# Layer 1's aggregation by pairs of panels: seven block products, weights behind each panel, clamp and residual on ScalarE

## The chip, the cores and the metric

The kernel runs on one NeuronCore of a Trainium2 chip. The metric is device time in microseconds (us) of one execution. The engines are named as the profile names them: PE (TensorE, matmul), DVE (VectorE), ACT (ScalarE), POOL (GpSimd) and SP (SyncE). ACT, POOL and SP also issue DMA transfers, each from a queue of its own that works in order.

## The reference

Two layers, each a graph aggregation followed by a mixture of experts with two of eight experts per node. There are 3327 nodes of 256 features in float32, and `adj` is 3327 x 3327 with about 0.24% of its entries nonzero, plus the diagonal.

```python
def _L1_gnn_ref(h, adj, simlar, W_proj, b_proj, W_gcn, b_gcn):   # simlar is adj
    sim = jnp.tanh(adj * simlar)
    filt = sim * (adj > 0).astype(sim.dtype)
    ...                                  # keep the 700 largest of a row
    h2 = jnp.tanh(h @ W_proj + b_proj)
    return jax.nn.relu(new_adj @ (h2 @ W_gcn) + b_gcn)
...
x = x + _L0_gnn_ref(_layernorm(x), adj, ...)     # relu(adj @ (x @ W) + b)
x = x + _L0_ffn_ref(_layernorm(x), ...)          # 8 experts, top 2, relu
x = x + _L1_gnn_ref(_layernorm(x), adj, adj, ...)
x = x + _L1_ffn_ref(_layernorm(x), ...)          # tokens + 8 experts, top 2, gelu
```

The last line adds its input twice: the experts of layer 1 return the normalized tokens plus the experts' sum, and x is added to that. So layer 1's x becomes x + xn before the outputs of the experts are added; this is called the residual below.

## The kernel before, in words

The nodes are padded to 3328: 26 tiles of 128, or 13 panels of 256. The transposed adjacency lies in memory as 13 panels of 256 columns, each panel in two pieces of 128 x 3328 (13 blocks of 128 rows each). Six places in SBUF, `ring`, hold pieces while they are used; `load_pieces` issues their loads on SP's queue in the order of `LOADS`, and the experts later use the same places for blocks of tokens and weights.

**Layer 0** (`aggregate_first`) aggregates the normalized features themselves and applies the weights afterwards: for every finished panel `weigh` (L506) does two matmuls a tile, then `add_relu` (L403, L404) adds bias and x on DVE. Panels 0 and 1 run together, panel 12 alone, and the ten between run as five pairs in `pair` (L571). Two panels, two halves of the nodes and two halves of the features make a 2 x 2 block product; `pair` does it with seven products of 13 matmuls each (L470) instead of eight, with sums of the features (`sum_features`, four DVE operations, once) and sums of pieces (`add_pieces`, L480, sixteen DVE operations a pair). While a pair runs, the panels of the pair before are weighed among the first product's matmuls, normalized, routed (`route`: DVE scores, L662) and listed (`listed`: tokens scattered to the experts' lists by POOL, small PE products L770 and L771). The normalized tiles come from ACT (L360).

**Between the layers** (`between`, L1635) each group of two tiles has the outputs of layer 0's experts added and is normalized on DVE (L1419, L337 to L371), transposed on PE (L387), copied by ACT, projected on PE (L1623) with tanh on ACT (L1630), and multiplied by the second weight in `node_features` (L395); ACT copies the result into `s` (L398). Behind the last normalized tiles the first pieces of layer 1 are filtered: DVE clamps a piece at zero (L1668), ACT squares it and takes tanh in quarters (L1672, L1673).

**Layer 1** (`aggregate`, L430) takes the 13 panels one at a time: 52 matmuls against `s` (L440), `add_relu`, then `after1`: list the panel before, normalize (DVE), scores (DVE; by PE for the last panel), and x + xn on POOL (L1690). `filter_chunk` filters each later piece when it is loaded: clamp on DVE (L1659), Square and Tanh on ACT (L1660, L1661). The exponential of the routing weights is ACT's too (L729).

**Experts of layer 1** run in steps: transposes (L1172), hidden layer (L1226), activation (ACT, L1234), output product (L1323), scaling on DVE (L1330, L1331), scatter to `ys` by POOL (L793). `first_blocks` starts with lists that `plan_early` closed after panel `EARLY_PANS[1]` (9 before). Once the outputs of the first experts are all written, an inner loop (L1762) loads them back while later steps run: `load_outputs` (L1405) on SP's queue, behind the loads of the next step's tokens and weights (L1136, L1143), then `add_loaded` on DVE (L1419) and the store of finished tiles on ACT's queue (L1769). The last tiles are stored at L1803.

Within an engine, instructions run in the order in which the program's scheduler left them; `behind(...)` and `tc.issue_after(...)` place an instruction later in that order.

Of the kernel before, what the change touches and what calls it, by code (L numbers as in the profile page):

```python
# [57 lines left out]
EARLY_PANS = 8, 9  # L58
# [9 lines left out]
def late_order(fixed, spread):  # L68
# [19 lines left out]
SIDE = 2  # L88
UNITS = (
    [(pan,) for pan in range(SIDE)] + [(pan, pan + 1) for pan in range(SIDE, NPAN - 1, 2)] + [(NPAN - 1,)],  # L90
    [(pan,) for pan in range(NPAN)],
# [36 lines left out]
def gnn_moe_two_layers(  # L128
# [262 lines left out]
    def node_features(i, lhsT, w_sb):  # L391

        ps = psy.tile([P, D], F32, name="ps_s", tag="py")
        for c in range(DC):
            nc.tensor.matmul(  # L395
                ps, lhsT=lhsT[:, c, :], rhs=w_sb[:, c, :], start=(c == 0), stop=(c == DC - 1)
            )
        nc.scalar.copy(s[:, i, :], ps)  # L398

# [29 lines left out]

    def aggregate(b_sb, prepare, after):  # L430

        load_pieces(RING - 2 * NCHUNK, prepare)
        for pan in range(NPAN):
            chunks = [piece(pan, k) for k in range(NCHUNK)]
            ps = [psy.tile([P, D], F32, name="ps_g", tag="py") for _ in range(PW // P)]
            for k in range(NCHUNK):
                for it in range(PW // P):
                    for c in range(CJ):
                        j = k * CJ + c
                        nc.tensor.matmul(  # L440
                            ps[it],
                            lhsT=chunks[k][:, c, ts(it, P)],
                            rhs=s[:, j, :],
                            start=(j == 0),
                            stop=(j == NT - 1),
                        )
            for it in range(PW // P):
                add_relu(x[:, pan * (PW // P) + it, :], ps[it], b_sb)
            after(pan)
            load_pieces(NCHUNK, prepare)  # L450
# [31 lines left out]
    def aggregate_first(b_sb, w, w_sb, begin, count, route, listed, freed):  # L482

        sums, waiting, copied, counts = {}, [], [], []
        units = UNITS[0]
# [22 lines left out]

        def finish():
            if not waiting:
                return
            todo = list(waiting)
            waiting.clear()
            if todo[0][0] < NPAN - 1:
                listed()
            for pan, g in todo:
                for it in range(PW // P):  # L520
                    weigh(pan, g, it)
            if todo[0][0] == NPAN - 1:
                listed()
            for _ in route([pan for pan, _ in todo]):
                pass
# [17 lines left out]
        def count_next():  # L543
            if counts:
                count(*counts.pop(0), copied)
# [11 lines left out]

        def rest(pan, first, hooks=(), behind_=BEHIND):
            hooks = dict(hooks)
            for j in range(first, NT):  # L560
                add(pan, j)
                if j == first + behind_:
                    finish()
                if j in hooks:
                    hooks[j]()
            g = sums_of()
            for c in range(DC):
                copy(g[:, c, :], sums[pan][c])
            waiting.append((pan, g))

        def pair(p1, p2, ps_x, ps_q, ps_b, ps_z):  # L571
            a11, a12, a21, a22 = (piece(pan, k) for pan in (p1, p2) for k in range(NCHUNK))
            b11, b21, b22 = half(0, 0), half(1, 0), half(1, 1)
            t3, t2, t4, t1 = half_sums
            hooks, pans = finishing()
            product(ps_x, b11, a11, hooks=hooks)
            g1, g2 = sums_of(), sums_of()
            copy(g1[:, 0, :], ps_x)
            add_pieces(a11, a21)
            add_pieces(a21, a22)  # L580
            count_next()
            listed()
            product(ps_q, t4, a22)
            copy(g2[:, 0, :], ps_q)
            routing = route(pans)
            next(routing)
            add_pieces(a22, a11)
            count_next()
            product(ps_b, b21, a12)
            nc.vector.tensor_tensor(g1[:, 0, :], g1[:, 0, :], ps_b, ALU.add)  # L590
            add_pieces(a12, a22)
            next(routing)
# [9 lines left out]
            count_next()  # L602
# [9 lines left out]

        expect(LOADS[0][SIDE:])
        counts.extend(LOADS[0][:SIDE])
        loads(2)
# [3 lines left out]
        loads(2)  # L619
        with tc.issue_after(last_piece[0].ins):  # L620
            turn_gate(f1_rT)
        for pan in range(SIDE):
            start(pan)
        for j in range(0, CJ, 2):
            for pan in range(SIDE):
                for i in range(j, min(j + 2, CJ)):
                    add(pan, i)
        for _ in range(SIDE):
            count_next()
        for pan in range(SIDE):  # L630
            free(pan, 0)
        for pan in range(SIDE):
            if pan == 1:
                begin(pan)
                sum_features()
            count_next()
            rest(pan, CJ)
            free(pan, 1)
        for _ in range(NCHUNK * SIDE):
            count_next()  # L640
        banks = [psy.tile([P, PW], F32, name="ps_g", tag="py") for _ in range(4)]
        for u in units[SIDE:-1]:
            begin(u[0])
            pair(*u, *banks)
            banks.append(banks.pop(0))
        sums[NPAN - 1] = banks[0:2]
        for _ in range(NCHUNK):
            count_next()
        rest(NPAN - 1, 0, {CJ: layer0.turn_first}, LAST_BEHIND)
        return finish  # L650

# [68 lines left out]
    def weights(sc, n, bias=None, now=False):  # L720


        if bias is not None:
            nc.vector.tensor_tensor(sc, sc, bias.unsqueeze(1).to_broadcast([P, n, E]), ALU.add)
        sel, top, both = top_two(sc, n)
        d = work.tile([P, n], F32, name="rt_d", bufs=2)
        nc.vector.tensor_tensor(d, top[:, :, 1], top[:, :, 0], ALU.subtract)
        if now:
            nc.scalar.activation(d, d, AF.Exp)  # L729
            return sel, both, shares(d, n)  # L730
        return sel, both, d
# [9 lines left out]
    def normalized(t, n, on_scalar=False):  # L741

        stats = statistics(t, n)
        if not on_scalar:
            return [layernorm(t + at, 2, stats, at) for at in range(0, n, 2)]
        shift = shifted(*stats, n)
        xns = [work.tile([P, 2, K, RW], F32, name="xn") for _ in range(0, n, 2)]
        for g in range(n):
            scaled(xns[g // 2][:, g % 2, 0, 0:D], t + g, g, stats[1], shift)
        return xns  # L750
# [4 lines left out]
    def list_waiting():  # L755
        while routed:
            list_tokens(*routed.pop(0))

    def list_tokens(xns, sel, both, w, t0, n, xlist, group):

        if group == "0":
            nc.scalar.activation(w, w, AF.Exp)
# [10 lines left out]
        if group == "0":  # L773
            w = shares(w, n)
# [629 lines left out]
    def load_outputs(yt, ys, t0, n, written, group=None):  # L1404
        d = nc.sync.dma_start(  # L1405
# [102 lines left out]
    def route0(pans):  # L1508
# [7 lines left out]
        routed.append((xns, *weights(sc, n, f0_bg_sb), t, n, xlist0, "0"))  # L1516

    def listed0():
        if not routed or len(routed) == 1 and routed[0][4] == 0:
            return  # L1520
        last = routed[-1][4] + routed[-1][5]
# [17 lines left out]
    layer0.step(None, between=finish_last)  # L1539
    layer0.step(None)  # L1540
# [76 lines left out]
    def second_features(t, xnT):  # L1617
# [13 lines left out]
        second.append(h2)  # L1631
        for g in range(n):
            node_features(t + g, h2T[:, :, ts(g, P)], g1_wg_sb)
# [22 lines left out]
    def filter_chunk(pan, k, a):  # L1656

        with behind(normal if pan == ahead else ()):
            nc.vector.tensor_scalar(a, a, 0.0, None, ALU.max)  # L1659
        nc.scalar.activation(a, a, AF.Square)  # L1660
        nc.scalar.activation(a, a, AF.Tanh)  # L1661
# [21 lines left out]
    def after1(layer1, pan):  # L1683
# [4 lines left out]
        routed.append((xns, *weights(sc, n, now=True), t, n, xlist1, "1"))  # L1688
# [8 lines left out]
    def panels1(layer1, turn=False):  # L1697


        def after(pan):  # L1700
            if pan < NPAN - 1:
                after1(layer1, pan)
                if turn and pan == NPAN - 2:
                    layer1.turn_first()
            else:
                list_waiting()

        return after

    def first_blocks(layer1):  # L1710
# [6 lines left out]
        layer1.step(None)  # L1717
        layer1.step(None)
        with tc.issue_after(last_product[0].ins):
            after1(layer1, NPAN - 1)  # L1720
        layer1.step(None)
# [10 lines left out]
    with tc.If(first_usual > 0) as arms:  # L1732
# [14 lines left out]
        aggregate(gnn_b_sb, filter_chunk, panels1(layer1, True))  # L1747
        late1 = first_blocks(layer1)
# [13 lines left out]
        with tc.If(second_usual > 0) as inner:  # L1762
# [8 lines left out]
            while len(layer1.started) < layer1.always:  # L1771
# [11 lines left out]
                if waiting and at > waiting[0][1] + (1 if k < FIRST_TILES // 2 else 2):  # L1783
                    tiles, _, written = waiting.pop(0)
                    yt = ring[k % RING][:, PIECE - 2 * K * D :].rearrange("p (n d) -> p n d", n=2)
                    load_outputs(yt, ys1, *tiles, written, "read1")
# [21 lines left out]
    with arms.Else():  # L1808
# [11 lines left out]
        with tc.If(most_reg > TOPK) as many:  # L1820
            with tc.tile_pool(name="topk", bufs=1) as tk:
                topk_rows(tc, tk, ring, psy, pst, adj, s, x, gnn_b_sb, ident, filtered, add_relu)
            for pan in range(NPAN):
                panels1(layer1)(pan)
        with many.Else():
# [4 lines left out]
            aggregate(gnn_b_sb, filter_chunk, panels1(layer1))  # L1830
        rows_written.extend(first_arm)
        early_rows.extend(first_arm)
        layer1.rest(first_blocks(layer1))
# [3 lines left out]
def topk_rows(tc, pool, places, psy, pst, adj, s, x, b_sb, ident, filtered, add_relu):  # L1837
# [8 lines left out]
    with tc.For_i(0, NT, 1) as i:  # L1846
# [49 lines left out]
        ps = psy.tile([P, D], F32, name="ps_k", tag="py")  # L1896
        for j in range(NT):
            nc.tensor.matmul(
                ps, lhsT=fT[:, j, :], rhs=s[:, j, :], start=(j == 0), stop=(j == NT - 1)
            )  # L1900
# [75 lines left out]
```

## Time and profile before

| | |
|---|---|
| device time, median of 3 runs | 1191.62 us (1187.46 to 1192.87) |
| profiled execution | 1192.74 us; span 1191.0 us, mean granted PE clock 0.989 |
| aggregation of layer 0, one pair | 43.02 us |
| first product of layer 1's aggregation | 748.68 us |
| one panel of layer 1 | 22.65 us |
| last product of layer 1's aggregation ends | 1043.8 us |
| last product of the experts ends | 1171.8 us |

Times inside an execution count from the start of its span. A row of a timeline gives start, duration, engine, line, operation, output and inputs, how many instructions were merged, and in brackets how long the engine had been idle before it and what ended that. A row of the windows gives, for a stretch of time, the busy time of each engine with the number of its instructions, then the clock granted to PE (1.00 is full), the busy share of the DMA engines and their GB/s. A row of the groups by form gives a line's instructions of one shape, their number, busy time, the mean of one in ns, and the idle time before them.

### The profile page before, as it was taken

How to read it: one execution, taken by the hardware profiler on the slowest of the kernel's cores; microseconds unless marked ns; L12 is line 12 of the kernel's file. 1: busy time of each engine (PE TensorE's matmuls, PEld its weight loads, DVE VectorE, ACT ScalarE, POOL GpSimd, SP SyncE). 2: the span in 40 equal slices, each digit the busy share in tenths (PEclk: the TensorE clock that was granted, in tenths of full speed). 3: DMA queues.
4: the chain of work that ended last, by engine and by line, in shares of the span. 5: the costliest groups of instructions: out<-in, count | busy, mean ns of one | idle time of the engine just before them, and what ended most of it. 6: DMA issues, size and time to landing. Idle time of an engine off the chain costs nothing. (4 is left out here: it accounts for less than half of the span.)

```text
span 1191.0 us, 19704 instructions
## 1 busy us (share of the span) xinstructions
PE 1152.0 (97%) x6217; PEld 1005.4 (84%) x6217; DVE 867.1 (73%) x3001; ACT 557.0 (47%) x1051; POOL 290.5 (24%) x367
## 2 busy tenths in 40 slices
PE   8999999999899999999999999999999999999973
PEld 7888888888788888888888888888888888888852
DVE  6698999988885555454545669289999998785454
ACT  5599647540233333434333346985455562043321
POOL 2111332242331112111111010022232232265531
PEclk9999999999999999999999999999999999999996
DMA  9896738724376555757565955145354451479696
GB/s 349 180 265 260 241 127 239 257 88 152 125 260 224 195 186 187 270 182 258 199 219 168 386 208 201 65 183 180 144 204 166 161 200 55 134 229 273 202 288 207
DMA packets 123185, 241.68 MB, mean 203 GB/s; under 512 B 24480, under 2 KB 93120, under 8 KB 116160
## 3 DMA queue, kind: packets, MB, share of 16 engines
q1 hardware_dynamic: 108656, 205.59, 52.7%
q0 software_dynamic: 11136, 31.60, 7.2%
q10 hardware_dynamic: 3280, 3.15, 0.8%
q8 instruction: 51, 0.84, 0.3%
q14 instruction: 62, 0.51, 0.1%
HBM read 203.98 MB, written 36.33 MB: 202 GB/s over the span
## 5 line engine op out<-in xcount | busy, mean ns | idle before, releaser
L440 PE MATMUL ps_g<-s,ring 128*128 128x256 f32 x1352 | 294.2, 380 | 0.0
L440 PEld LDWEIGHTS ps_g<-s,ring 128*128 128x128 f32 x1352 | 256.0, 190 | 34.4
L1234 ACT ACTIVATE pad<-ps_h,ring 128x256 f32<-128x256 f32 (+1 forms) x282 | 128.9, 458 | 287.2 <-PE ps_h L1226 156.1
L1226 PE MATMUL ps_h<-pad,ring 128*128 128x256 f32 (+1 forms) x1184 | 254.4, 367 | 4.4 <-ACT pad L1176 4.1
L1226 PEld LDWEIGHTS ps_h<-pad,ring 128*128 128x128 f32 x1184 | 200.9, 190 | 46.7 <-ACT pad L1234 11.1
L662 DVE SCALAR_TENSOR_TENSOR rt_product<-xn,gate 128x256 f32<-128x256 f32 x400 | 194.9, 487 | 16.1 <-ACT xn L360 2.8
L793 POOL DMA_INDIRECT ys<-pad,index x114 | 115.7, 1015 | 363.8 <-DVE pad L1281 236.1
L793 POOL DMA_INDIRECT xlist<-xn,rt_idx x104 | 115.0, 1106 | 156.9 <-DVE ln_nw L347 60.9
L1495 ACT ACTIVATE sign<-ring,below 128x416 bf16<-128x416 f32 x208 | 133.4, 641 | 13.8 <-DMA ring<-in_adjT 7.8
L470 PE MATMUL ps_g<-ring,pad 128*128 128x256 f32 x520 | 115.1, 380 | 0.8 <-DMA ring<-in_adjT 0.8
L470 PEld LDWEIGHTS ps_g<-ring,pad 128*128 128x128 f32 x520 | 98.4, 190 | 14.4 <-DMA ring<-in_adjT 1.2
L1660 ACT ACTIVATE ring<-ring 128x3328 f32<-128x3328 f32 x22 | 65.4, 2979 | 87.3 <-DVE ring L1659 56.2
L1281 DVE SCALAR_TENSOR_TENSOR pad<-ps_y,ring,pad 128x128 f32<-128x128 f32 x176 | 59.3, 348 | 47.5 <-PE ps_y L1274 47.3
L470 PE MATMUL ps_g<-ring,s 128*128 128x256 f32 x390 | 89.6, 379 | 0.0
L470 PEld LDWEIGHTS ps_g<-ring,s 128*128 128x128 f32 x390 | 74.1, 190 | 10.1
L480 DVE TENSOR_TENSOR ring<-ring,ring 128x768 f32<-128x768 f32 (+1 forms) x80 | 79.7, 1014 | 0.0
L495 PE MATMUL ps_g<-ring,s 128*128 128x256 f32 x312 | 70.2, 386 | 4.4 <-ACT s L360 4.4
L495 PEld LDWEIGHTS ps_g<-ring,s 128*128 128x128 f32 x312 | 60.1, 194 | 13.5 <-ACT s L360 5.2
L1661 ACT ACTIVATE ring<-ring 128x3328 f32<-128x3328 f32 x22 | 65.4, 2979 | 0.6
L1265 DVE TENSOR_TENSOR xnT<-pad 128x512 f32<-128x512 f32 x22 | 15.2, 692 | 59.2 <-ACT pad L1234 59.2
L1323 PE MATMUL ps_y<-ring,pad 128*128 128x256 f32 x224 | 53.8, 386 | 0.0
L776 POOL COPY xn<-rt_w 128x4 f32<-128x4 f32 x26 | 4.8, 198 | 197.8 <-DVE rt_w L738 197.8
(240 smaller groups left out, 1584.3 us busy)
## 6 DMA issues: line engine op xcount, KB each, us to landing
ring<-in_adjT SPq DMA_DIRECT2D x50, 1664.0 KB, 8.2
ring<-in_f_w1T SPq DMA_DIRECT2D x30, 1024.0 KB, 5.7
ring<-in_f_w2T SPq DMA_DIRECT2D x30, 1024.0 KB, 8.0
ring<-xlist SPq DMA_DIRECT2D x52, 258.0 KB, 3.5
ring<-in_f_w SPq DMA_DIRECT2D x36, 256.0 KB, 3.8
ring<-ys SPq DMA_DIRECT2D x12, 512.0 KB, 4.2
ring<-in_f_b SPq DMA_DIRECT2D x34, 128.0 KB, 7.6
xlist<-h2T SPq DMA_DIRECT2D x16, 257.0 KB, 7.8
```

What stands on the lines that cost most here:

```text
L440: nc.tensor.matmul(ps[it], lhsT=chunks[k][:, c, ts(it, P)], rhs=s[:, j, :], start=(j == 0), stop=(j == NT - 1),)
L470: nc.tensor.matmul(ps, lhsT=b[:, c, :], rhs=a[:, c, :], start=(first and c == 0), stop=(c == CJ - 1), skip_group_check=not first,)
L480: nc.vector.tensor_tensor(out[:, part, :], out[:, part, :], other[:, part, :], ALU.add)
L495: nc.tensor.matmul(sums[pan][c], lhsT=s[:, j, ts(c, P)], rhs=piece(pan, j // CJ)[:, j % CJ, :], start=(j == 0), stop=(j == NT - 1),)
L662: nc.vector.scalar_tensor_tensor(product, xn, 1.0, gate[:, e, :], ALU.mult, ALU.mult, accum_out=sc[:, g, e : e + 1],)
L793: d = nc.gpsimd.indirect_dma_start(out=a[:, :], out_offset=bass.IndirectOffsetOnAxis(ap=index, axis=0), in_=rows_, in_offset=None,)
L1226: last_product[:] = [nc.tensor.matmul(ps, lhsT=w1[:, c, ts(hc, P)], rhs=xT[:, c, :], start=(c == 0), stop=(c == DC - 1),)]
L1234: nc.scalar.activation(hT[:, hc, :], ps, func, bias=bb1[:, hc : hc + 1])
L1281: last_y[:] = [nc.vector.scalar_tensor_tensor(part, ps, xb[:, g, WT : WT + 1], part, ALU.mult, ALU.add)]
L1495: nc.scalar.activation(sign, piece(pan, k)[:, :, ts(i, GROUP)], AF.Sign, bias=below, accum_out=positive[:, pan, i, k : k + 1],)
L1660: nc.scalar.activation(a, a, AF.Square)
L1661: nc.scalar.activation(a, a, AF.Tanh)
```

## The change

It has seven parts.

1. `aggregation` is cut out of `aggregate_first`, and `aggregate_second` uses it for layer 1: panels 0 to 9 as five pairs, panels 10, 11 and 12 alone. The aggregated thing is h2 itself; `weigh` multiplies by the weight behind each panel, so `second_features` transposes h2 back by tiles (four transposes and one copy for two tiles) where `node_features` multiplied. `sum_features` runs for layer 1 too.
2. In the first pair (`begun`) the product of b21 and a12 comes second and the one of t4 and a22 third; the other pairs keep layer 0's order.
3. `filter_piece` clamps on ACT (Relu), then Square and Tanh; of one piece in each pair DVE clamps half.
4. In pairs ACT writes the normalized tiles and also x + xn (`twice`: x scaled by the inverse deviation plus one); panels alone keep DVE and POOL.
5. Routing is spread: `route1` is a generator, the exponential moves to `shares_begun`, lists are done one at a time (`list_next`) at set places (`LIST_AT`, `FURTHER_AT`); the last panel is weighed and routed inside the first three expert steps. `EARLY_PANS` is 8, 8. Panels 11 and 12 take their scores from PE. At the end of layer 0's aggregation the second-last list moves behind the first expert step.
6. The inner loop's `load_outputs` goes to ACT's queue.
7. `topk_rows`, an arm that these inputs don't take, is fitted to the new order of products.

```diff
-EARLY_PANS = 8, 9
+EARLY_PANS = 8, 8
...
-SIDE = 2
+SIDE, ALONE = 2, 3
+LIST_AT, FURTHER_AT = (6, 22, 14), (12, 12, 18)
 UNITS = (
...
-    [(pan,) for pan in range(NPAN)],
+    [(pan, pan + 1) for pan in range(0, NPAN - ALONE, 2)] + [(pan,) for pan in range(NPAN - ALONE, NPAN)],
 )
...
+        def pair(p1, p2, ps_x, ps_q, ps_b, ps_z, filtering=False, begun=False):
...
+            def second_sum():
+                product(ps_q, t4, a22)
+                copy(g2[:, 0, :], ps_q)
+
+            def first_output():
+                product(ps_b, b21, a12)
+                nc.vector.tensor_tensor(g1[:, 0, :], g1[:, 0, :], ps_b, ALU.add)
+
...
+            if begun:
+                first_output()
+            else:
+                second_sum()
             routing = route(pans)
-            next(routing)
+            next(routing, None)
+            if begun:
+                second_sum()
             add_pieces(a22, a11)
             count_next()
-            product(ps_b, b21, a12)
-            nc.vector.tensor_tensor(g1[:, 0, :], g1[:, 0, :], ps_b, ALU.add)
+            if not begun:
+                first_output()
...
+    def aggregate_second(b_sb, w_sb, count, route, listed, freed, turn_first=None):
+
+        a = aggregation(UNITS[1], b_sb, w_sb, count, route, listed, freed)
+        a.loads(RING - 2 * NCHUNK)
+        sum_features()
+        banks = banks_of_pairs()
+        pairs = [u for u in UNITS[1] if len(u) == 2]
+        for u in pairs:
+            a.pair(*u, *banks, filtering=True, begun=u is pairs[0])
+            banks.append(banks.pop(0))
+        for i, pan in enumerate(range(NPAN - ALONE, NPAN)):
...
+            hooks[BEHIND] = weighed
+            hooks[LIST_AT[i]] = listed
+            hooks[FURTHER_AT[i]] = further
+            hooks[NT - 3] = ended
...
+        if twice:
+            more = work.tile([P, n], F32, name="ln_more", bufs=2)
+            nc.vector.tensor_scalar(more, stats[1], 1.0, None, ALU.add)
+            for g in range(n):
+                scaled(x[:, t + g, :], t + g, g, more, shift)
...
+        pt = psy.tile([P, n, D], F32, name="ps_s", tag="py")
         for g in range(n):
-            node_features(t + g, h2T[:, :, ts(g, P)], g1_wg_sb)
+            for c in range(DC):
+                nc.tensor.transpose(pt[:, g, ts(c, P)], h2T[:, c, ts(g, P)], ident)
+        nc.scalar.copy(s[:, t : t + n, :], pt)
...
-    def filter_chunk(pan, k, a):
-
-        with behind(normal if pan == ahead else ()):
-            nc.vector.tensor_scalar(a, a, 0.0, None, ALU.max)
-        nc.scalar.activation(a, a, AF.Square)
-        nc.scalar.activation(a, a, AF.Tanh)
+    def filter_piece(pan, k, copied):
+
+        a = piece(pan, k).rearrange("p c w -> p (c w)")
+        shared = pan < NPAN - ALONE and pan % 2 == 0 and k == 1
+        parts = [a[:, 0 : PIECE // 2], a[:, PIECE // 2 :]] if shared else [a]
+        if shared:
+            nc.vector.tensor_scalar(parts[1], parts[1], 0.0, None, ALU.max)
+        with behind(copied):
+            nc.scalar.activation(parts[0], parts[0], AF.Relu)
+            nc.scalar.activation(a, a, AF.Square)
+            nc.scalar.activation(a, a, AF.Tanh)
...
-                    load_outputs(yt, ys1, *tiles, written, "read1")
+                    load_outputs(yt, ys1, *tiles, written, "read1", nc.scalar)
```

## The prediction

> **What bounds the kernel now.** I read the page's busy times first, then the busy time by stage, then the seams in the timelines.
>
> The page, busy time of each engine:
>
> ```profile
> PE 1152.0 (97%) x6217; PEld 1005.4 (84%) x6217; DVE 867.1 (73%) x3001; ACT 557.0 (47%) x1051; POOL 290.5 (24%) x367
> ```
>
> TensorE (PE) sets the time nearly everywhere. The windows show where another engine is close behind (a layer-0 pair; the end of the stage between the layers; two stretches of layer 1's aggregation; the last expert steps):
>
> ```profile
> core 0: us, PE busy (x) PEld busy (x) DVE busy (x) ACT busy (x) POOL busy (x), PEclk, DMA share, GB/s
> ...
> 144.00:187.00 43.00, 43.00 (x208) 37.79 (x207) 40.32 (x134) 26.58 (x74) 12.55 (x14) 1.00 0.52 186
> ...
> 725.00:750.00 25.00, 24.51 (x122) 20.41 (x122) 21.40 (x51) 18.97 (x38) 0.59 (x2) 1.00 0.38 137
> 750.00:775.00 25.00, 25.00 (x117) 22.02 (x116) 5.72 (x16) 25.00 (x29) 0.00 (x0) 1.00 0.26 87
> ...
> 900.00:925.00 25.00, 25.00 (x121) 21.94 (x120) 22.90 (x86) 14.46 (x7) 6.39 (x8) 1.00 0.51 193
> ...
> 1125.00:1150.00 25.00, 20.86 (x103) 16.39 (x102) 15.49 (x42) 7.67 (x15) 9.70 (x10) 1.00 0.90 289
> 1150.00:1175.00 25.00, 18.41 (x100) 15.33 (x99) 12.80 (x40) 7.37 (x20) 9.91 (x10) 0.93 0.77 243
> ```
>
> Layer 0's pairs, which the change copies, already have DVE at 40.32 of 43. ACT is full just where layer 1's first pieces are filtered (25.00 of 25). PE has real holes only in the last two rows, where the DMA engines are 0.90 and 0.77 busy.
>
> PE's timeline, at a stall in layer 0 and where layer 1's aggregation starts:
>
> ```profile
> 311.67 0.17 PE L770 MATMUL pr<-rt_both,before 128*128 128x8 bf16 x1 [3.07 <-DVE rt_both L700]
> ...
> 311.75 1.09 PE L1172 MATMUL ptb<-ident,ring 128*128 128x128 f32 x4
> ...
> 748.68 0.59 PE L440 MATMUL ps_g<-s,ring 128*128 128x256 f32 x2
> ```
>
> After 3.07 idle, four transposes take 1.09 where 0.60 is usual: the idle costs some 1.75 more in slow instructions until 315.7. DVE's and ACT's timelines at the same seam:
>
> ```profile
> 738.42 5.49 DVE L1668 TENSOR_SCALAR ring<-ring 128x3328 f32<-128x3328 f32 x3
> ```
>
> ```profile
> 739.99 1.68 ACT L1672 ACTIVATE ring<-ring 128x832 f32<-128x832 f32 x2
> ...
> 770.95 0.90 ACT L1673 ACTIVATE ring<-ring 128x832 f32<-128x832 f32 x1
> ```
>
> DVE runs without a gap from 707 to 747.5; ACT filters four pieces from 739.99 to 771.7.
>
> DVE's and ACT's groups by form, layer 1's panels (775 to 1035):
>
> ```profile
> L662 DVE SCALAR_TENSOR_TENSOR rt_product<-xn,gate 128x256 f32<-128x256 f32 x192 | 103.6, 540 | 5.8
> L1659 DVE TENSOR_SCALAR ring<-ring 128x3328 f32<-128x3328 f32 x19 | 35.7, 1880 | 0.0
> ```
>
> ```profile
> L1661 ACT ACTIVATE ring<-ring 128x3328 f32<-128x3328 f32 x21 | 62.4, 2979 | 0.6
> ```
>
> The expert tail, one stall followed from DVE to ACT to PE, and the SP queue's waits from 1119 to 1163:
>
> ```profile
> 1133.20 0.69 DVE L1419 TENSOR_TENSOR x<-x,ring 128x512 f32<-128x512 f32 x1 [3.06 <-DMA ring<-ys]
> ```
>
> ```profile
> 1134.65 0.38 ACTq L1769 DMA_DIRECT2D out_x<-x  x1
> ```
>
> ```profile
> 1135.77 1.99 PE L1226 MATMUL ps_h<-pad,ring 128*128 128x256 f32 x8 [2.57 <-ACT pad L1176]
> ```
>
> ```profile
> SPq L1405 <- DMA ys<-pad,index: 15.4, 5, 5.1
> ```
>
> A load of expert outputs comes late, DVE's add waits, the store behind it holds ACT, ACT's copy holds PE.
>
> **PE's work, by count.** A 128x256 f32 matmul costs 0.4357 us (the 52 of a panel fill 22.65). Panels alone: 13 x 52 = 676. After: five pairs of 7 x 13 = 91, three panels of 52: 611. The difference, 65, is -28.3. The weight product leaves the stage between the layers (52 matmuls, in its place 52 transposes at 0.108) and comes back behind the panels: +22.7. What the stage between gains is not 22.7, because DVE sets its pace from 707 on (8.06 per four tiles); its last normalized tiles come at 738.5, about 1.8 later with one feature sum (1.88 in layer 0) put among them. So the first product starts about 743.4 instead of 748.68: -5.3.
>
> **The first pair** is a new wait. Its second product in PE's order is b21 with the piece that ACT filters last; before, a panel needed its two pieces 11.3 us apart and ACT made one in 6.3. Rows: ACT took 739.99 to 771.74, less one whole 2.87 piece that lay between, less 1.1 for fewer copies: 27.8. It can start at about 736.7, when the shorter PE work lets the third-last features through, so the fourth piece is done at 764.5 and its first quarter (0.785 an operation, six before the end) at 759.8. PE finishes its first product at 749.5, waits 10.3, and ends the second at 765.9 where 755.2 was possible: +10.7. Bounds: +9 if the filter starts right after its clamp, +15 if it starts at 739.99 as now. The slow clock after it: the row at 311.75 says +1.75.
>
> **The steady pairs.** PE needs 43.02 each. DVE in a layer-0 pair takes 43.38 from one last addition (L605, 146.09) to the next (189.47) with 1.0 of idle, so 42.4 of work and issue; layer 1 adds half a clamp (0.95) and 0.2 of scale, and the waits for ACT's normalized tiles (0.72 there): 43.5 to 44.1. The third weight product leaves about 2.1 of slack, so four pairs cost 0 to +2.3; I take +1. ACT has 11.5 filter operations of 2.87, eight scaled tiles of 0.45 and four copies: 38 to 39 of 43. Moving the clamp to ACT looks wrong by operation, 2.98 against 1.88, but four clamps on DVE would add 7.2 to a DVE that has 0.6 left. The Trainium skill, "ScalarE: Activation LUTs", section "Rules for kernel authors", says that relu and max belong on VectorE and not on ScalarE; the rows agree on the price of one operation, but by that rule each pair would run at some 49.6, so I go by the row of the pair. The residual leaves POOL for ACT; with it goes what stretches L662 here (540 ns against 446 in a layer-0 pair), which is why I use layer 0's rows for DVE.
>
> **Panels alone, seams.** Panel 11 now takes its scores from PE as panel 12 does (transposes 0.43, products 0.89 at 1053.11): +1.3, and hides nothing. The last panel's weights (1.74, within the 22.7) move into the expert steps. The exponential no longer switches ACT's function just before a needed activation (PE waited 1.00 at 1060.27), and the seam at 311 lists later: together -1.0, at best -4, at worst 0. The earlier plan (panel 8) only frees loads that were not late.
>
> **The tail.** On SP the loads stood before the next expert's tokens and weights; on ACT's queue they stand before the next hidden activations. Removed: 2.57 + 1.20 + 0.37 + 3.08 of PE waits and 1.6 of slow clock after the last (1.87 for 1.05 and 1.71 for 1.03), 8.8. Added: ACT now waits for the scatter that SP waited for (3.1, 5.1, 2.4, 1.4, 3.4), with 2.0 idle before each activation as cover: 1.1 + 3.1 + 0.4 + 0 + 1.4, about 5, and what stands behind it is PE. So -4; bounds -8.8 and +5. The Trainium skill, "Trainium Kernel Development and Optimization", section "Key Constraints", says that transfers from all queues share the same 16 DMA engines, so that another issuing engine saves only issue time. By that rule alone the term is near 0 with the share at 0.90; the 0.56 share in 1120 to 1125, while SP was blocked, says that something is left to gain.
>
> **Sum.** -28.3 + 22.7 - 5.3 + 10.7 + 1.75 + 1 + 1.3 - 1.0 - 4 = -2.1. The profiled execution took 1192.74 (span 1191.0), so 1190.6; it lies 1.1 above the median, so 1189.5.
>
> **Rivals.**
> - Faster: the tail frees itself wholly. All 8.8 go (-4.8 more), and the last output loads, eight queued on SP from 1163.68 with the final one taking 6.33, become four (a ys load takes 2.7 at best: -3.6). That gives 1181. For it: PE idles 4.1 in the first tail window alone. Against: the DMA share.
> - Slower, the pace of pairs: DVE's scores wait for normalized tiles that stand on ACT behind a 2.98 operation, once a pair, so a pair takes 46.0 and four cost 12 where I took 1: 1200.5. It decides from the point where DVE needs more than 43.6 a pair. For it: DVE at 40.32 of 43 before the addition. Against: only 0.72 of such waits in layer 0.
> - Slower, ACT blocked in the tail: nothing of the 8.8 goes since the DMA engines are full, and 5 come on top: 1198.5.
>
> **Chances.** Within 0.5% (6 us, about what a measurement can tell) by the forecast: 0.40, own range 1184 to 1196. Tail freed: 0.33. Pace: 0.16. ACT blocked: 0.11. The forecast's low end gives some to faster, and the two slow cases reach below +6 a little: faster 0.36, same 0.39, slower 0.25. The range takes in the fast case with the short bound of the wait (1176) and the pace case with 2.5 over it (1203).
>
> **What would show it.** A PE gap of about 10 in the first pair released by ACT; pairs at 43 to 44; DVE's L662 back near 446 ns; aggregation ending at 1043 to 1047; ys loads on ACT's queue with PE waits of 1 to 3 behind them. Wrong if the first pair has no gap, or if pairs take 45 or more, or if the tail is shorter by over 9.

## The result, and the profile after

| | before | after |
|---|---|---|
| device time, median of 4 runs each | 1190.15 us (1187.46 to 1192.87) | 1249.31 us (1241.07 to 1251.06) |
| ratio | | 1.0494, 95% interval 1.044 to 1.0548 |
| profiled execution; span; mean granted clock | 1192.74; 1191.0; 0.989 | 1251.06; 1249.3; 0.966 |
| layer 0's aggregation ends | 299.97 | 302.07 |
| first projection between the layers | 698.42 | 705.13 |
| first product of layer 1's aggregation | 748.68 | 751.79 |
| last product of it ends | 1043.99 | 1090.78 |
| last product of the experts ends | 1171.82 | 1233.07 |

The change makes the kernel 4.9% slower, where the prediction said no difference. From one row of the table to the next the loss is 2.1 (a wait for an early load of adjacency, 0.85 before and 3.11 after, which took from nothing to 3.11 in the traces of the runs), 4.6, -3.6, 43.7 and 14.5, and the end after the last product is 3.0 shorter: together 58.3, the difference of the spans. The page's busy times of after:

```profile
PE 1155.3 (92%) x6151; PEld 1000.9 (80%) x6151; DVE 859.2 (69%) x2896; ACT 637.7 (51%) x1122; POOL 285.4 (23%) x357
```

PE has 66 instructions fewer than before and is busy 3 us longer, since more of them run at a slower clock; the other 55 us are idle time of PE. PE's timeline shows where it stands in the aggregation (the first pair, three later pairs, a panel alone). The profile counts two instructions for a matmul, so x26 is one product of 13 matmuls. The third and fourth rows were read in windows that end inside them; in full they are x26 and take 7.73 and 8.53:

```profile
767.77 8.08 PE L440 MATMUL ps_g<-ring,s 128*128 128x256 f32 x26 [9.88 <-ACT ring L1748]
...
886.05 8.66 PE L440 MATMUL ps_g<-ring,s 128*128 128x256 f32 x26 [7.36 <-ACT xnT L509]
...
939.14 6.22 PE L440 MATMUL ps_g<-ring,s 128*128 128x256 f32 x19 [7.01 <-ACT xnT L509]
...
992.14 8.09 PE L440 MATMUL ps_g<-ring,s 128*128 128x256 f32 x24 [7.86 <-ACT xnT L509]
...
1066.61 3.78 PE L472 MATMUL ps_o<-g_wg_sb,xnT 128*128 128x256 f32 x8 [4.48 <-ACT xnT L509]
```

The first row is the wait for the filtered piece that was forecast. The next three were not: they come once a pair, and PE waits for L509, ACT's copy of a finished sum out of PSUM, the memory that PE writes its sums to. The pairs with these gaps last 53.43, 52.15 and 53.80; the second pair, which has none, lasts 42.99. The windows of two of them (start and end, length, busy time of PE, of its weight loads, of DVE, ACT and POOL, granted clock, DMA share, GB/s):

```profile
846.70:900.20 53.50, 46.14 (x208) 39.75 (x208) 42.64 (x147) 41.84 (x27) 10.13 (x14) 0.90 0.42 149
900.20:952.30 52.10, 45.09 (x207) 39.04 (x206) 40.81 (x135) 38.76 (x26) 10.64 (x14) 0.93 0.43 152
```

No engine is full. All of them wait for something, and PE's clock falls with it (0.90, 0.93). ACT's timeline ahead of the first of these gaps:

```profile
871.18 1.08 ACT L361 ACTIVATE xn<-x,ln_shift,ln_guess 128x256 f32<-128x256 f32 x2
873.14 2.96 ACT L1736 ACTIVATE ring<-ring 128x3328 f32<-128x3328 f32 x1
883.67 1.09 ACT L361 ACTIVATE xn<-x,ln_shift,ln_guess 128x256 f32<-128x256 f32 x2 [7.57 <-DMA xlist<-xn,rt_idx]
885.65 0.62 ACT L509 COPY xnT<-ps_g 128x256 f32<-128x256 f32 x2
```

POOL's timeline beside it, the first and the last of eight scatters:

```profile
871.44 0.98 POOL L858 DMA_INDIRECT xlist<-xn,rt_idx  x1 [0.81 <-DVE ln_more L796]
...
880.82 0.97 POOL L858 DMA_INDIRECT xlist<-xn,rt_idx  x1 [0.30 <-issue]
```

Read backwards: PE waits for the copy at 885.65; the copy stands on ACT behind the second half of a pair's normalized tiles at 883.67; that waits for a DMA that reads `xn`, a scatter of the pair before. `xn` has three buffers of two tiles and a pair takes two, so a pair's second one needs a buffer of the pair before, which is free only when its tokens have been scattered. In layer 0 the lists stand before the second product of a pair (`listed` in `pair`); for layer 1 the change puts them behind the third, so the scatters issue only from 871.44 to 881.79. ACT asks for the buffer at 876.10 (the end of the row at 873.14), four scatters have to land for it, and it goes on at 883.67. The late issue is not all of it: the scatters now also run beside the load of an adjacency piece that SP issued at 873.15. The one issued at 871.44 landed after 2.9, the one at 874.00 after 9.2, at 883.24. ACT's groups by form sum it up for the aggregation (775 to 1065; shape, count, busy time, mean ns, idle time before it and its releasers):

```profile
L361 ACT ACTIVATE xn<-x,ln_shift,ln_guess 128x256 f32<-128x256 f32 x20 | 10.8, 589 | 28.1 <-DMA xlist<-xn,rt_idx 22.9 <-issue 3.3 <-DVE ln_more L796 2.0
```

22.9 us of ACT's time go to that one wait.

The rest of the loss lies elsewhere. In layer 0's experts PE has a new wait for tokens; the SP queue shows their load, which stood at 330.08 before:

```profile
348.50 0.63 PE L1237 MATMUL ptb<-ident,ring 128*128 128x128 f32 x4 [3.21 <-DMA ring<-xlist]
```

```profile
345.05 0.38 SPq L1201 DMA_DIRECT2D ring<-xlist  x1
```

In the last expert steps ACT now waits for the scatters of expert outputs (ACT's waits, 1130 to 1245: total, times, longest), and PE for ACT:

```profile
ACT pad L1299 <- DMA ys<-pad,index: 22.1, 6, 4.8
```

```profile
1209.62 0.69 PE L1237 MATMUL ptb<-ident,ring 128*128 128x128 f32 x2 [2.54 <-ACT pad L1299]
...
1223.93 0.44 PE L1237 MATMUL ptb<-ident,ring 128*128 128x128 f32 x2 [2.25 <-ACT pad L1299]
...
1231.94 1.13 PE L1388 MATMUL ps_y<-s,pad 128*128 x4 [3.54 <-ACT pad L1299]
```

### The profile page after: what moved, and what is told of

It reads as the page before. It is cut to its first block, busy times and chain, and to the rows that moved or that the text cites. A ratio compares the mean times of both kernels' runs of the same rounds, so it can differ in the third digit from the quotient of the medians.

```text
span 1249.3 us, 19591 instructions
## 1 busy us (share of the span) xinstructions
PE 1155.3 (92%) x6151; PEld 1000.9 (80%) x6151; DVE 859.2 (69%) x2896; ACT 637.7 (51%) x1122; POOL 285.4 (23%) x357
## 5 line engine op out<-in xcount | busy, mean ns | idle before, releaser
L440 PE MATMUL ps_g<-ring,pad 128*128 128x256 f32 x1040 | 231.6, 382 | 3.1 <-DMA ring<-in_adjT 3.1
L440 PEld LDWEIGHTS ps_g<-ring,pad 128*128 128x128 f32 x1040 | 198.1, 191 | 30.5 <-DMA ring<-in_adjT 3.5
L440 PE MATMUL ps_g<-ring,s 128*128 128x256 f32 x780 | 189.0, 394 | 32.1 <-ACT xnT L509 22.2
L440 PEld LDWEIGHTS ps_g<-ring,s 128*128 128x128 f32 x780 | 154.4, 199 | 56.9 <-ACT xnT L509 23.8
L709 DVE SCALAR_TENSOR_TENSOR rt_product<-xn,gate 128x256 f32<-128x256 f32 x384 | 168.8, 440 | 37.2 <-ACT xn L361 23.3
L450 DVE TENSOR_TENSOR ring<-ring,ring 128x768 f32<-128x768 f32 (+1 forms) x160 | 159.0, 1013 | 2.5 <-ACT ring L1748 1.3
L461 PE MATMUL ps_g<-ring,s 128*128 128x256 f32 x624 | 139.1, 382 | 4.3 <-ACT s L361 4.3
L461 PEld LDWEIGHTS ps_g<-ring,s 128*128 128x128 f32 x624 | 118.7, 192 | 21.2 <-ACT s L361 4.8
L1734 ACT ACTIVATE ring<-ring 128x3328 f32<-128x3328 f32 (+1 forms) x22 | 59.9, 2721 | 2.3 <-DMA ring<-in_adjT 2.3
L509 ACT COPY xnT<-ps_g 128x256 f32<-128x256 f32 x52 | 18.5, 363 | 82.9 <-PE ps_g L440 56.9
L1388 PE MATMUL ps_y<-ring,pad 128*128 128x256 f32 x224 | 56.4, 400 | 0.0
```

The costliest lines, as they stand in the source:

```text
L440: nc.tensor.matmul(ps, lhsT=b[:, c, :], rhs=a[:, c, :], start=(first and c == 0), stop=(c == CJ - 1), skip_group_check=not first,)
L450: nc.vector.tensor_tensor(out[:, part, :], out[:, part, :], other[:, part, :], ALU.add)
L461: nc.tensor.matmul(sums[pan][c], lhsT=s[:, j, ts(c, P)], rhs=piece(pan, j // CJ)[:, j % CJ, :], start=(j == 0), stop=(j == NT - 1),)
L709: nc.vector.scalar_tensor_tensor(product, xn, 1.0, gate[:, e, :], ALU.mult, ALU.mult, accum_out=sc[:, g, e : e + 1],)
L1734: nc.scalar.activation(parts[0], parts[0], AF.Relu)
```

## The experiments

The runs came from four chips, on which the kernel before took 1188.1, 1204.3, 1190.5 and 1206.9 us; each ratio is against the kernel before on the same chip. The expectations in us assume a chip where the kernel before takes some 1190.

**Lists early in every pair.** The theory above, against the rival that ACT is simply overloaded.

```diff
-            if not filtering:
-                listed()
+            listed()
             if begun:
...
-            if filtering:
-                listed()
             product(ps_z, t1, a21)
```

> Layer 1's pairs list the previous pair where layer 0's pairs do, before the second product, so that POOL's scatters release the normalized tiles some 11 us earlier. Theory 1 (three buffers for normalized tiles, and the third pair's second tile waits for the scatters of the pair before): the PE gaps of 7.36, 7.01 and 7.86 us in pairs 3 to 5 go, pairs come to 43 to 44 us, and the time falls by about 30 us to some 1219. Theory 2 (ACT simply has too much to do since clamp and residual moved there, so its copies of the products come late): the gaps stay, pairs stay near 53, the time near 1249.

Measured: 1217.9 us, ratio 1.0244 (1.0214 to 1.0275). PE's timeline at the places of the old waits:

```profile
878.96 5.88 PE L440 MATMUL ps_g<-ring,s 128*128 128x256 f32 x26 [0.62 <-ACT xnT L509]
...
966.13 5.88 PE L440 MATMUL ps_g<-ring,s 128*128 128x256 f32 x26 [0.86 <-ACT xnT L509]
...
1037.86 3.55 PE L472 MATMUL ps_o<-g_wg_sb,xnT 128*128 128x256 f32 x8 [4.39 <-ACT xnT L509]
```

Where 7 us were, 0.62 and 0.86 are left, and the pairs take 43 to 44. ACT is busy for nearly as long as in the changed kernel (39.04 and 38.26 in two windows of 44, against 41.84 and 38.76 in the two windows above), so the rival falls. The scatters, issued from 861.9 on and mostly ahead of the next load of a piece (872.79), now land in 3.1 (median), where 8.3 was measured in the changed kernel. By the ratios, the place of the lists cost about 30 of the 59 us. The wait before a panel alone stays.

**A fourth buffer.** The same theory from the other side: the lists stay late, `xn` gets four buffers, and smaller pools make room.

```diff
-        xns = [work.tile([P, 2, K, RW], F32, name="xn") for _ in range(0, n, 2)]
+        xns = [work.tile([P, 2, K, RW], F32, name="xn", bufs=4) for _ in range(0, n, 2)]
...
-        t = work.tile([P, D], F32, name="gnn_t", bufs=2)
+        t = work.tile([P, D], F32, name="gnn_t", bufs=1)
...
```

> Four buffers for normalized tiles instead of three, lists where the changed kernel has them (room is made by letting scratch tiles that only DVE uses share their places). Theory 1: the waits of ACT's L361 for xlist scatters go, pairs come to 43 to 44 us, some 1219 us, as when the lists are moved. Theory 2: nothing changes, 1249.

Measured: 1226.86 us, ratio 1.0323 (1.0281 to 1.0366). Of the three waits 0.40 and 0.63 are left, and none at the first place:

```profile
926.06 5.88 PE L440 MATMUL ps_g<-ring,s 128*128 128x256 f32 x26 [0.40 <-ACT xnT L509]
...
969.98 5.88 PE L440 MATMUL ps_g<-ring,s 128*128 128x256 f32 x26 [0.63 <-ACT xnT L509]
```

The scatters still land late here (median 7.5 between 846 and 890), so a free buffer was what ACT waited for. It gains less than the early lists. The stage between the layers is 3.9 longer than in the changed kernel (50.55 against 46.66), presumably for the smaller pools.

**The clamp of later pieces on DVE.**

```diff
-        if shared:
-            nc.vector.tensor_scalar(parts[1], parts[1], 0.0, None, ALU.max)
+        nc.vector.tensor_scalar(a, a, 0.0, None, ALU.max)
         with behind(copied):
-            nc.scalar.activation(parts[0], parts[0], AF.Relu)
```

> The clamp of all later pieces goes back to DVE (6.7 us less of ACT work a pair net, about 6.3 more of DVE). Theory 2: ACT's copies come in time, pairs fall below 50 us and the time by 10 or more. Theory 1: the gaps of pairs 3 to 5 stay at 7 us or grow, since ACT still stops at the same buffer, and pairs that had no gap (the second) become longer than 43; 1249 or slower.

Measured: 1246.33 us, ratio 1.0487 (1.0439 to 1.0535), no gain. PE's three old waits are gone, and it waits for DVE at the weights of the next pair instead:

```profile
906.44 2.08 PE L472 MATMUL ps_o<-g_wg_sb,xnT 128*128 128x256 f32 x4 [4.71 <-DVE gnn_t L395]
...
956.37 2.08 PE L472 MATMUL ps_o<-g_wg_sb,xnT 128*128 128x256 f32 x4 [4.20 <-DVE gnn_t L395]
```

These rows, one pair apart, are 49.93 apart. The prediction had worked out 49.6 for a pair with its clamps on DVE, but this is no confirmation, since DVE is not full: from 856.5 to 956.4, two pairs, it is busy for 87.7 of 99.9 and waits 7.5 for normalized tiles from ACT. ACT in turn waits longer for the scatters than in the changed kernel, 37.5 against 22.9 (775 to 1065: total, times, longest):

```profile
ACT xn L361 <- DMA xlist<-xn,rt_idx: 37.5, 4, 13.5
```

So the first theory holds, that ACT stops at the same buffer, though PE's wait moved.

**The first pair in layer 0's order.**

```diff
-            a.pair(*u, *banks, filtering=True, begun=u is pairs[0])
+            a.pair(*u, *banks, filtering=True, begun=False)
```

> The first pair of layer 1 keeps the order of the others: the product of t4 and a22 second, the one of b21 and a12 (the piece filtered last) third. If the 9.88 us gap of the first pair is only the wait for the fourth piece, the second product can start once the third piece is filtered, about 6.3 us earlier: gap 3 to 4 us, and with a shorter spell of slow clock 6 to 8 us less in all, 1242. Rival: t4 comes late from DVE (its sums end at 759.9) or the additions to a22 then come late, and the gap only moves: 1249.

Measured: 1241.9 us, ratio 1.0446 (1.0416 to 1.0476). PE's wait in the first pair falls from 9.88 to 4.00:

```profile
761.26 8.83 PE L440 MATMUL ps_g<-ring,pad 128*128 128x256 f32 x26 [4.00 <-ACT ring L1748]
```

So the special order of the first pair, part 2 of the change, costs some 4 to 6 us by itself: the wait is 5.9 shorter, the aggregation 4.4 (334.56 against 338.99), and the ratios differ by 0.5%, within their intervals.

**Layer 0's last lists where they were.**

```diff
     layer0.step(None, between=finish_last)
-    with tc.issue_after(last_product[0].ins):
-        list_next()
     layer0.step(None)
...
```

> The last lists of layer 0 stand where the kernel before had them: one before the last panel is routed, none behind the first expert step. Theory: the third step's tokens are loaded at 345 instead of 330 because their scatters start at 333 instead of 318; with the lists back the wait of 3.21 us at 348.5 and its slow clock go, the wait of 3 us at 311 gets its slow products back, and layer 1 starts 4 to 5 us earlier: 1244 to 1245. Rival (the load is late for another reason, the early plan of panel 8): the wait at 348 stays, 1249.

**Loads of expert outputs back on SP.**

```diff
-                    load_outputs(yt, ys1, *tiles, written, "read1", nc.scalar)
+                    load_outputs(yt, ys1, *tiles, written, "read1")
```

> The inner loop's loads of expert outputs go back to SP's queue, all else as changed. From the fifth expert step to the end the kernel before takes 128.5 us and the changed one 134.2. If ACT's waits for scatters (in front of its activations) are the cause, the stretch returns to 128 to 130 and the time falls by 4 to 6, to 1244. If the freed SP queue is worth its 4 us as forecast and the stretch is long for another reason, it becomes longer: 1253.

**The kernel before with only these loads on ACT's queue.**

```diff
...
-                    load_outputs(yt, ys1, *tiles, written, "read1")
+                    load_outputs(yt, ys1, *tiles, written, "read1", nc.scalar)
```

> The kernel before with that one part of the change: loads of expert outputs on ACT's queue. ACT-waits theory: 4 to 6 us slower, 1194. The forecast of the prediction: 4 us faster, 1184 to 1186. If the DMA engines' throughput sets the stretch alone: the same.

These three ran on one chip: 1253.81 us (ratio 1.0416, 1.0345 to 1.0488), 1248.82 (1.0389, 1.0329 to 1.0449) and 1210.29 (1.0046, 1.0019 to 1.0073). On a chip where the kernel before takes 1190 these ratios would be some 1240, 1236 and 1196 (an estimate): the first two lie below the 1244 of their theories, the first within its interval, and the third is as the theory of ACT's waits had it. By stage: from the end of layer 0's aggregation to the first projection they take 402.84, 408.18 and 403.58; only the second has the moved list, which costs 5.3; with the list back the wait of 3.21 for tokens is gone, as expected. From the end of layer 1's aggregation to the last product they take 147.5, 136.8 and 147.6; only the second has the loads on SP. Between the first two, 9.4 of the 10.7 lie behind the fourth expert step, where these loads are, and 1.3 come back after the last product, so in these two profiles ACT's queue costs some 8. The 147.6 is no measure of it: ahead of the first of these loads (1137.74) PE already waits 1.26, 2.96 and 3.30, where the kernel before on the first chip has one wait of 1.00. By the medians of one chip, in the kernel before, where nothing else changes, the queue costs 0.46%, some 5.5 us (2.3 to 8.7). Two timelines of that kernel at one load, ACT with its queue and then PE:

```profile
1143.93 0.38 ACTq L1405 DMA_DIRECT2D ring<-ys  x1
1144.41 0.47 ACT L1234 ACTIVATE pad<-ps_h,f_b_sb 128x256 f32<-128x256 f32 x1 [4.23 <-DMA ys<-pad,index]
```

```profile
1144.94 0.66 PE L1172 MATMUL ptb<-ident,ring 128*128 128x128 f32 x4 [1.98 <-ACT pad L1234]
```

The load does not issue before the scatter has landed, the activation behind it has 4.23 of idle time before it for a transfer that it has no use for, and PE waits for the activation.

**The four amendments together** (lists early, the first pair's order, layer 0's lists, SP's queue).

> The four at once: lists early in layer 1's pairs, second sum before first output in the first pair, layer 0's last lists and the queue of the loads as before. If the parts add: 1249.3 - 31 - 7 - 4.5 - 5 = 1201 to 1202, still slower than before by 1%, since the stage between the layers keeps DVE's pace, and the panels alone and the first expert steps keep their waits (4.4 at panel 11's weights, about 6 in the first steps). If there is one bound behind them all (ACT in order), less is gained: 1208 or more.

Measured: 1209.94 us, ratio 1.0047 (1.0023 to 1.0072); at 1190 before that is some 1196, less than the sum of the parts. The places of three groups of instructions and the queue of one group of loads account for some 53 of the 59 us. The products by pairs remain in this version, and bring no gain.

**Scores of panel 10 on PE as well**, on top of the four.

```diff
-        if alone and pans[0] > NPAN - ALONE:
+        if alone and pans[0] >= NPAN - ALONE:
```

> The version with the four amendments, and panel 10 too takes its scores from PE. Theory (the 4.32 us before panel 11's weights are ACT's PSUM copies standing behind an exponential that waits for DVE's scores of panel 10): the gap goes, 4.3, with some 1 of slow clock after it, and 1.3 of transposes and products comes on PE: about 4 us less than the version with the four amendments, which stood 5.6 us above before, so a ratio of 0.998 to 1.003. Rival (DVE is late there by itself, whoever makes the scores): the gap only changes its releaser to DVE, ratio 1.005 or more.

Measured: 1203.76 us, ratio 1.0108 (1.0083 to 1.0132). The wait of 4.3 is gone, as the theory had it, but no time is won, as the rival had it: PE's timeline has a longer wait, for DVE, in its place.

```profile
1011.72 1.09 PE L388 MATMUL pt<-ident,xn 128*128 128x128 f32 x4 [8.95 <-DVE xn L372]
```

DVE normalizes panel 10's tiles behind the scores of the last pair; the transposes of these tiles, put at a fixed place on PE, wait for that, and all that stands behind them on PE waits too. The aggregation takes 310.25, against 304.45 with the four amendments alone.

**The last panel routed at once**, on top of that.

```diff
             with tc.issue_after(last_product[0].ins):
-                next(routing[0])
-            layer1.step(None, between=ended)
+                for _ in route1(routing[0]):
+                    pass
+            layer1.step(None)
```

> As the run before, and the last panel is normalized, routed and scored at once after the second expert step, as in the kernel before (its weights stay in the first step). Theory (the gaps of 0.52, 0.35, 0.91, 1.32 and 2.04 in the first expert steps come from the last panel's routing spread over them): they go in part, 2 to 5 us less than the run before. Rival (they come from ACT's and DVE's load there, wherever the routing stands): no difference within 1.5 us.

Measured: 1203.41 us, ratio 1.0116 (1.0092 to 1.0139), no difference. The last experts take 130.9, against 132.3.

**The kernel before once more**, for its trace on the chip of these two.

> The kernel before itself, for its trace on the chip of these runs: first aggregation product near 748, aggregation ending 295 later, last product of the experts 128 to 141 after that. If the experts take 128 here, the amended version still loses about 9 there; if they take 135 or more, it loses little there.

Measured: 1186.91 us, a single run; the aggregation takes 295.3 and the last experts 125.96. Against it the version of the run above loses about 5 in the experts, all of it in the first four steps (23.6 against 18.5; from there to the last product they take 107.3 and 107.5). Of this 1.7 are the last panel's weights and 2.2 waits (1.18 and 1.00 for ACT and 1.06 for DVE, against one of 1.00); about 1 is left for slow instructions. After the last product it loses 2.6 more.

**Panel 10's transposes later**, on top of the version with the last panel routed at once.

```diff
-LIST_AT, FURTHER_AT = (6, 22, 14), (12, 12, 18)
+LIST_AT, FURTHER_AT = (6, 22, 14), (12, 23, 18)
...
-            hooks[NT - 3] = ended
+            hooks[NT - 1 if i == 1 else NT - 3] = ended
```

> As the version with panel 10's scores by PE and the last panel routed at once, but panel 10's transposes stand eleven sum steps later in panel 11 (after matmul group 23 instead of 12) and its scores behind them. Theory (the 8.78 us before those transposes are PE waiting in order for a tile that DVE normalizes only after the 64 score operations of the last pair): the wait goes and nothing takes its place, 8.8 us and some 1 to 2 of slow clock less: a ratio of 1.001 to 1.005 where that version had 1.0116. Rival (the wait moves on to the next thing that needs DVE, panel 11's weights or panel 10's list): 4 us or less, ratio above 1.007.

Measured: 1208.21 us, ratio 1.0013 (0.9991 to 1.0035), level with the kernel before on the same chip. The same transposes, and no wait:

```profile
1020.55 0.60 PE L388 MATMUL pt<-ident,xn 128*128 128x128 f32 x4
```

From 986 to 1049.9 PE is busy without a break, and the aggregation takes 297.9, against 309.2 in the version that this one changes. No version beats the kernel before.

## Why the prediction was wrong, step by step

- **The sum** does not add up. Its nine terms give -1.15, not -2.1, and the waits that the tail adds (1.1 + 3.1 + 0.4 + 0 + 1.4) are 6.0, not about 5, which makes that term -2.8. Set right, the forecast is some 1191.7 instead of 1189.5, still no difference; this is not what failed. Nor does the low end of the range follow from its terms: 1181 less 1.7 for the shorter wait is 1179, not 1176.
- **PE's work by count** held. With the predicted terms the amended aggregation is 295.3 - 28.3 + 21.0 (weights without the last panel's) + 1.3 = 289.3; the last version takes 297.9, and 6.5 of the 8.6 between them are its wait of 3.64 in the first pair, 1.8 of slow clock behind it and a wait of 1.04 in a later pair, and 1.3 the scores of panel 10, which the prediction had not put on PE.
- **First product earlier**, -5.3: the stage between took 46.66 instead of 50.26, so -3.6. Right in kind.
- **The first pair**, +10.7 and +1.75: a gap of 9.88, and the product behind it in 8.08 instead of 5.78, 12.2 in all. Right, for the reason given. The prediction did not ask whether the order that it priced was the better one: with layer 0's order the wait is 4.0.
- **The steady pairs**, +1, is the step that failed. It asked how much work each engine has in a pair and found 0.6 of slack on DVE and 4 on ACT. That part is right: with the lists early, pairs take 43 to 44, as forecast. It did not ask when a buffer comes free. The lists' move within the pair was not costed at all, nor its scatters on POOL, though these release `xn`, which ACT fills, and ACT also copies PE's sums. Nor did it ask what runs beside the scatters at their new place. Three pairs took 159.4 instead of 129.1, +30.3. DVE's scores did fall back as forecast, to 437 ns from 804 to 1006.
- **The rival on the pace of pairs** had the place (DVE waiting for normalized tiles once a pair) and not the cause: it put the tiles behind a filter operation of 2.98, at 46.0 a pair; they stood behind a scatter, at 52 to 54. Its deciding point, DVE over 43.6 a pair, was not what decided.
- **Panels alone**, +1.3 "and hides nothing": from 1006.11 to 1090.78 they took 84.7, where 67.95 of products, 6.97 of weights and 1.3 make 76.2. Of the difference 4.48 is PE's wait for a copy that stands on ACT behind an exponential, which waits for DVE's scores of panel 10; most of the rest is slow clock (0.88 from 1066.6 on). The runs on that place show DVE late there whichever engine makes the scores.
- **Seam of layer 0**, within the -1.0: the stall of 3.07 at 311 stayed as one of 2.96 at 313.66, another of 3.21 came at 348, and 4.6 were lost by the first projection. The list that moved took its scatters along, and the next step's tokens are loaded behind them.
- **The tail**, -4 with +5 as its bad end: +5.7 for the steps from the fifth on with what the shorter end gives back, and +5.8 in the first four, of which the sum held only the last panel's weights. In the kernel before, the queue alone costs 5.5, about the bad end and the rival on ACT. What failed is the gain set against ACT's new waits: 8.8 of PE's idle time and slow clock were to go, but with the queue moved PE's gaps over 1 us from 1144 on add up to 8.9 (without one of 2.06 for which the profile shows no releaser), where before, on another chip, had 6.9.
- **The rules.** The Trainium skill, "ScalarE: Activation LUTs", section "Rules for kernel authors", puts relu and max on VectorE. For one operation the rows agree, 1920 ns on DVE (with all clamps there) against 2976 on ACT. The 49.6 that the prediction set against this rule for a pair is not shown: the pairs of 49.9 have late lists, and DVE waits in them. Without its waits, 10.3 in the two pairs, DVE needs some 45 a pair there (99.9 less 10.3, halved, an estimate); clamps on DVE with the lists early were not run. The Trainium skill, "Trainium Kernel Development and Optimization", section "Key Constraints", leaves another issuing engine only the issue time to save. No run here contradicts that, but its term near 0 was too kind: the 5.5 come from what ACT cannot do while the load ahead of it waits.

The range ended at 1203 because its bounds came from waits that the trace of before holds; a wait that only the new order creates is in no row of it. What stays open: what clamps on DVE would cost with the lists early, why ACT and DVE are late in the first expert steps of the amended kernel, and whether the last version, level on a chip where before takes 1206.9, is level where it takes 1190.

## What to carry to other kernels

When a step moves, write down for each buffer it reads who fills it next, and where that engine stands in its own order: with three buffers and two taken a round, a release that comes after the next request stops an engine that has work. Look also at which transfers the moved step's own transfers will run beside. Where no engine is full and the bottleneck idles once a round, follow the releasers back to the transfer that holds the buffer. Put a load that waits for a late transfer on the queue of an engine with nothing to compute behind it.

## What the runs showed of the hardware

- A gap cost more than its length. After PE had idled 7.36, the next product took 8.66 instead of 5.88 (granted clock 0.76 from 885 to 899), and the pair lost 10.4 in all; the prediction knew 1.75 after a gap of 3.07. The extra does not grow with the gap: behind gaps of 3.64 (the last version), 4.00 (the first pair in layer 0's order), 7.36 and 9.88 (the changed kernel) a product took 7.58, 8.83, 8.66 and 8.08.
- The scatters landed later than before. From issue to landing, minimum, median and maximum between 860 and 890 in the changed kernel, for those of the eight scatters whose landing the trace holds:

```profile
DMA to landing us min/median/max: 2.9/8.3/9.2
```

Between 855 and 890 the median was 4.8 before. It goes with the loads of adjacency pieces beside them: from 871 to 885 the DMA engines are 0.79 busy and the median is 8.3; with the lists early, from 861 to 877, they are 0.35 busy, and the median is 3.1. No run changes the loads alone.
- The kernel before took 1188 to 1207 us on four chips, a wider spread than most of the differences sought here. The aggregation of layer 1 took 295.3 in all three traces of it (one with the loads on ACT's queue); the stretch from the end of layer 0's aggregation to the first projection took 398.5, 396.8 and, on the chip with 1204.3, 403.6.
